# Two down projections of an f32 feed-forward kernel: the order of the operand forms in one, a second level of block products in the other

## The chip, the cores and the metric

The kernel runs on one core of a Trainium2 chip. The core has a matrix engine (TensorE, "PE" in the profile, with its weight loads as "PEld"), a vector engine (VectorE, DVE), a scalar engine (ScalarE, ACT), a general engine (GpSimd, POOL) and a queue engine (SyncE, SP). Each takes its instructions in order from a queue of its own, and they meet through semaphores. On-chip data lies in SBUF (128 partitions); TensorE writes its results into eight PSUM banks of 128 x 512 f32.

The metric is the device time of one launch in microseconds. The kernel before takes 685.91 us, the median of three runs (685.76 to 686.01).

## What is computed

1024 tokens (8 batches of 128) with 512 features pass through two residual layers. Cut to what matters:

```python
x = x + _L0_ffn_ref(_L0_cond_ref(x, ...), ...)     # 1: conditioner, then feed-forward
x = x + _L1_ffn_ref(_L1_cond_ref(x, ...), ...)     # 2: conditioner, then int4 feed-forward

def _L0_cond_ref(x, ...):                           # F = 1376, low-rank adapters of rank 16 by batch
    gate = lora_add(einsum('bnh,fh->bnf', x, W_gate), x, A_gate, B_gate)
    up   = lora_add(einsum('bnh,fh->bnf', x, W_up), x, A_up, B_up)
    act  = silu(gate) * up
    return lora_add(einsum('bnf,hf->bnh', act, W_down), act, A_down, B_down)

def _L0_ffn_ref(x, ...):                            # I = 1792, weights scaled by a rank-4 product
    d = silu(linear(x, gate_w, ...)) * linear(x, up_w, ...)
    return linear(d, down_w, ...)
```

The change concerns the two products with the down weights: `act` times `W_down` of the conditioner (1376 inputs, padded to 11 chunks of 128; 512 outputs; 1024 tokens), and `d` times `down_w` of the feed-forward (14 chunks of 128).

## The kernel before

**Layout.** Features lie on the 128 partitions, tokens on the free axis, so a matmul takes a 128 x 128 weight block (128 inputs, 128 outputs) and streams up to 512 tokens. Tokens come in two halves of 512 (`tb` 0 and 1), the 512 outputs in four blocks of 128 (`o`, or `m` and `m + 2` for the two halves of the outputs). Everything in these layers is f32.

**Seven products in place of eight.** Each projection is a 2 x 2 block product: inputs in two halves, outputs in two halves, tokens in two halves. It is made by the Winograd form of Strassen's scheme. With weights a11, a12, a21, a22 and tokens b11, b12, b21, b22, where the even chunks of the inputs are one half and the odd chunks the other, there are weight forms S1 = a21 + a22, S2 = S1 - a11, S3 = a11 - a21, S4 = a12 - S2, token forms T1 = b12 - b11, T2 = b22 - T1, T3 = b22 - b12, T4 = b21 - T2, and the products

- 1: a11 b11, 2: a12 b21, 3: S4 b22, 4: a22 T4, 5: S1 T1, 6: S2 T2, 7: S3 T3.

Outputs are sums of these; in the code products 2 and 3 are added by TensorE to the banks of 1 and 5, the others by DVE, ACT and POOL. A product is, for `m` in 0 and 1, one matmul of 128 x 512 per pair of chunks: 5 pairs in the conditioner (10 matmuls a product), 7 in the feed-forward (14). The conditioner's eleventh chunk has no partner; its products are made straight (`leftover`), and its low-rank adapters are added to the banks (`adapters`).

**The conditioner's down part** is `down` (L601), with `n = 11`. Forms are made on DVE: S1 of each pair at L302 while `weight_forms` is called with `later`, T3 into tiles of their own (`dt_c`, through `form`, L622 to L627), then T1, T2, T4 in place on the activations; the later weight forms S2, S4, S3 at L309, pair by pair (128 x 256). Product order: 1, the low-rank block of the down adapters (hook 1, tile `pt_d`), 2, 5, 3, 7, 6, 4. ACT copies product 1 to `du_c` (L672), products 2 and 3 to the output `h` (L669, L683), product 7 to `dv_c` (L701), POOL adds `dv_c` to `h` (L704), DVE adds the rest (L656, L707, L709, L710). Hook 6 makes the token forms of the next projection (L336) in the tiles `x`, whose contents are no longer needed by then; `x` is loaded again much later for the residual.

**The feed-forward's down part** is `down_second` (L716), with 14 chunks. Products 1, 5 and 6 are made as above. Products 2, 3, 7 and 4 go down one more level: six of their seven pairs are again a 2 x 2 block product (two groups of three pairs, two output blocks, two quarters of 256 tokens), made as seven parts of three matmuls of 128 x 256 (`of_blocks`, `part`), and the last pair is added with two matmuls of 128 x 512. The block that the second level shares (`z`, in bank `z1`) is copied by ACT after the parts 1, 6 and 7 (L809, L813, L817) into `r`; parts 6 and 7 add to the same bank after the copy before them. Their token forms come from DVE (`second_tokens`, L760), their weight forms from POOL (`second_weights`, through L302 and L309). DVE's order, written out by hand (L834 to L872): seven T3 after S1 of all pairs in one instruction, seven T1, then S2, S4, S3 of all pairs (128 x 1792), the tokens of product 2, of product 3, and so on. POOL gathers the adapters of the last conditioner and makes its weight forms in hook 2, after the weight forms of product 7; hook 3 turns scales on TensorE ahead of product 7. PE's order: 1, 5, 2, 3, 7, 6, 4.

**What sets the order.** Matmuls and most forms are wrapped in `in_order`, which keeps the order of the program on their engine; the rest is placed by a scheduler. Banks are eight, taken by `bank`; a bank is free when its last reader is done. After both down parts come the last conditioner (tiles `l`) and the int4 feed-forward (`gu_q`, `d_q`), whose weights POOL's queue loads (`load_q`, L1399 and L1401).

Of the kernel before, what the change touches and what calls it, by code (L numbers as in the profile page):

```python
# [7 lines left out]
F32 = mybir.dt.float32  # L8
# [3 lines left out]
ALU = mybir.AluOpType  # L12

P = 128
NB = 8
T = 1024
TB = 512
# [38 lines left out]
def kernel(  # L56
# [544 lines left out]
    def down(pool, layer: str, n: int, to, plus: bool, hooks, adapters=None):  # L601

        pairs = n // 2
        K2 = KC // 2
        blocks = {"11": 0, "12": 1, "21": 2, "22": 3}
        b = {
            w: [acts[2 * j + i // 2, i % 2] for j in range(pairs)] for w, i in blocks.items()  # L610
        }
        a = {i: [] for i in range(1, 8)}
        forms = []
        for j in range(pairs):
            wd = [ready[layer, "down", 2 * j + i] for i in range(2)]
            s = pool.tile([P, 3, H // 2], F32, tag=f"ds{j}", name=f"ds_{layer}{j}")
            halves = [w[:, bass.ts(i, H // 2)] for i in range(2) for w in wd]
            forms.append(weight_forms(nc.vector, *halves, *(s[:, i] for i in range(3)), True, later=True))
            for i, w in zip((1, 2, 7, 4, 5, 6, 3), (*halves, *(s[:, i] for i in range(3)))):
                a[i].append([w[:, bass.ts(m, P)] for m in range(K2)])  # L620

        def form(t: str, x1: str, x2: str, place):  # L622
            b[t] = []
            for j in range(pairs):
                out_ = place(j)
                in_order(nc.vector.tensor_tensor(out_, b[x1][j], b[x2][j], ALU.subtract))
                b[t].append(out_)  # L627

        def at(o: int, tb: int):
            return to[o][:, bass.ts(tb, TB)]  # L630

        banks = {}

        def sums(i: int, m: int, src: str, into=None, start=True, single=None, stop=True, goes_on=False):


            ps = banks[i, m] = bank(f"d{i}_{layer}{m}") if into is None else into
            alone = single is not None and n % 2
            product(ps, [w[m] for w in a[i]], b[src], start, stop and not alone, goes_on)
            if alone:  # L640
                leftover(ps, m, *single, False, stop, goes_on)
            return ps

        def leftover(ps, m: int, row: int, tb: int, start: bool, stop: bool, goes_on=False):
            wd = ready[layer, "down", n - 1]
            mm(
                ps, wd[:, bass.ts(m + 2 * row, P)], acts[n - 1, tb], start=start, stop=stop,
                skip_group_check=goes_on,
            )

        def hook(i: int):
            if i in hooks:
                hooks[i]()

        def plus_bank(o: int, tb: int, ps):
            nc.vector.tensor_tensor(at(o, tb), ps, at(o, tb), ALU.add)  # L656

        def temp(what: str, m: int):
            return pool.tile([P, TB], F32, tag=f"{what}{m}", name=f"{what}_{layer}{m}")

        u = [temp("du", m) for m in range(2)]
        v = [temp("dv", m) for m in range(2)]
        more = adapters is not None
        form("T3", "22", "12", lambda j: pool.tile([P, TB], F32, tag=f"dt{j}", name=f"dt_{layer}{j}"))
        def moved(o: int, tb: int, ps):
            if plus:
                plus_bank(o, tb, ps)
            else:
                nc.scalar.copy(at(o, tb), ps)  # L669

        for m in range(2):
            nc.scalar.copy(u[m], sums(1, m, "11"))  # L672
        hook(1)
        form("T1", "12", "11", lambda j: b["12"][j])
        for rest in forms:
            rest()
        for m in range(2):
            ps = sums(2, m, "21", banks[1, m], False, (0, 0), not more, True)
            if more:
                extra = bank(f"d8_{layer}{m}")  # L680
                leftover(extra, m, 1, 1, True, False)
                adapters(m, [[ps, None], [None, extra]], go_on={(0, 0)})
                nc.scalar.copy(at(m + 2, 1), extra)  # L683
            moved(m, 0, ps)
        for m in range(2):
            plus_bank(m + 2, 1, sums(5, m, "T1"))
        hook(5)
        for m in range(2):
            ps = sums(3, m, "22", banks[5, m], False, (0, 1), not more, True)
            if more:  # L690
                banks[4, m] = bank(f"d4_{layer}{m}")
                adapters(
                    m, [[None, ps], [banks[4, m], None]], fresh={(1, 0)}, more={(1, 0)},
                    go_on={(0, 1)},
                )
            moved(m, 1, ps)
        form("T2", "22", "T1", lambda j: b["22"][j])
        form("T4", "21", "T2", lambda j: b["21"][j])
        for m in range(2):
            ps = sums(7, m, "T3")  # L700
            nc.scalar.copy(v[m], ps)  # L701
            if plus:
                nc.gpsimd.tensor_tensor(at(m + 2, 0), at(m + 2, 0), v[m], ALU.add)
            nc.gpsimd.tensor_tensor(at(m + 2, 1), at(m + 2, 1), v[m], ALU.add)  # L704
        for m in range(2):
            ps = sums(6, m, "T2")
            nc.vector.tensor_tensor(u[m], ps, u[m], ALU.add)  # L707
            for o in (m, m + 2):
                nc.vector.tensor_tensor(at(o, 1), at(o, 1), u[m], ALU.add)  # L709
            nc.vector.tensor_tensor(at(m + 2, 0), at(m + 2, 0) if plus else v[m], u[m], ALU.add)  # L710
        hook(6)
        for m in range(2):
            ps = sums(4, m, "T4", banks.get((4, m)), not more, (1, 0))
            plus_bank(m + 2, 0, ps)

    def down_second(pool, act, hooks):  # L716

        pairs, thirds, quarter = NF // 2, NF // 4, TB // 2
        K2 = KC // 2
        ds = pool.tile([P, pairs, 3, H // 2], F32, tag="ds", name="ds_f")
        dt = pool.tile([P, pairs, TB], F32, tag="dt", name="dt_f")
        wd = [[wd_all[:, i::2, bass.ts(row, H // 2)] for i in range(2)] for row in range(2)]
        a = {
            1: wd[0][0], 2: wd[0][1], 7: wd[1][0], 4: wd[1][1],
            5: ds[:, :, 0], 6: ds[:, :, 1], 3: ds[:, :, 2],
        }  # L730
        b = {f"{i + 1}{tb + 1}": act[:, i::2, tb] for i in range(2) for tb in range(NTB)}
        b["T3"], b["T1"], b["T2"], b["T4"] = dt, b["12"], b["22"], b["21"]
        other_forms = weight_forms(nc.vector, *wd[0], *wd[1], *(a[i] for i in (5, 6, 3)), True, later=True)

        def form(t: str, x1: str, x2: str):
            for j in range(pairs):
                in_order(
                    nc.vector.tensor_tensor(b[t][:, j], b[x1][:, j], b[x2][:, j], ALU.subtract)  # L738
                )


        tokens2 = pool.tile([P, 4, thirds, quarter], F32, tag="tokens2", name="tokens2_f")
        own = [tokens2[:, i] for i in range(4)]
        b11 = [
            b["11"][:, i * thirds : (i + 1) * thirds, bass.ts(q, quarter)]
            for i in range(2) for q in range(2)
        ]
        groups = [slice(i * thirds, (i + 1) * thirds) for i in range(2)]
        second = {}

        def second_tokens(i: int, src: str, place, in_place: bool):

            b11, b12, b21, b22 = (
                b[src][:, group, bass.ts(q, quarter)] for group in groups for q in range(2)
            )
            t1, t2, t4, t3 = place
            if in_place:
                t3 = b12
            for to, x1, x2 in ((t1, b12, b11), (t2, b22, t1), (t4, b21, t2), (t3, b22, b12)):
                in_order(nc.vector.tensor_tensor(to, x1, x2, ALU.subtract))  # L760
            second["b", i] = {1: b11, 2: b21, 3: b22, 4: t4, 5: t1, 6: t2, 7: t3}

        def second_weights(i: int):
            a11, a12, a21, a22 = (
                a[i][:, group, bass.ts(m, P)] for m in range(2) for group in groups
            )
            s = pool.tile([P, 3, thirds, P], F32, tag="s2", name=f"s2_{i}", bufs=2)
            s1, s2, s4 = (s[:, n] for n in range(3))
# [3 lines left out]
        def at(o: int, tb: int):  # L772
            return x[o][:, bass.ts(tb, TB)]
# [1018 lines left out]
```

## Time and profile before

| | us |
|---|---|
| median of three runs | 685.91 (685.76 to 686.01) |
| the profiled execution, its own time | 684.2 |
| its span, first to last instruction | 682.4 |
| conditioner's down part on PE | 156.72 to 233.88 |
| feed-forward's gate and up on PE | 233.88 to 400.84 |
| feed-forward's down part on PE | 400.84 to 486.81 |
| last conditioner on PE | 486.81 to 517.89 |
| int4 feed-forward | 517.89 to the end |
| mean granted TensorE clock | 0.995 of full speed |

The profile is one execution. It gives busy time by engine, the chain of work that ended last, groups of equal instructions with their duration and the idle time before them, and a timeline. A matmul's end is modelled, so the distance between two starts is the safer duration. An f32 matmul of the program shows as two records. "x20" is a merged run of twenty records, and the bracket at the end of a line is the idle time of the engine before it and what ended it. In the stretches of 78 us around the conditioner's down part (156 to 234) DVE is busy 34.36 us, ACT 6.89 and POOL 2.53; from 430 to 490 DVE is busy 46.48 and POOL 45.11.

### The profile page before, as it was taken

The page shows a single profiled execution, that of the slowest core. Times are in us where ns is not written, and L with a number is a line of the kernel's source. Part 1 is how long each engine was busy: PE and PEld are TensorE (multiplying, and loading weights), DVE is VectorE, ACT ScalarE, POOL GpSimd, SP SyncE. Part 2 cuts the span into 40 slices and gives each one's busy share as a digit, 9 for nine tenths or more (in the row PEclk, how much of TensorE's full clock was granted, in tenths as well). Part 3 has the DMA queues.
Part 4 walks back from the last instruction along what each step waited for, and adds up shares of the span by engine and source line. Part 5 has one row for each costly group of instructions (what it writes and reads, how often), then busy time and mean ns, then how long its engine had stood idle before and what let it go on. Part 6 is the DMA issues. An engine that isn't in the chain of part 4 may idle for free.

```text
span 682.4 us, 7042 instructions
## 1 busy us (share of the span) xinstructions
PE 669.2 (98%) x2472; PEld 397.0 (58%) x2472; DVE 471.8 (69%) x637; ACT 189.7 (28%) x282; POOL 390.8 (57%) x343
## 2 busy tenths in 40 slices
PE   9999999999999999999999997999999999999995
PEld 3444444444444445666666653685636877788884
DVE  6545435434523586877878679886857888899997
ACT  1212112111101012334323320010114555656563
POOL 5357765340001045667866921488721998898996
PEclk9999999999999999999999998999999999999999
DMA  7501225030002002202200060000670130000003
GB/s 236 195 1 52 66 76 212 28 138 1 1 0 77 32 0 92 93 6 87 93 1 0 1 205 1 0 13 4 213 249 6 57 94 15 16 1 0 1 1 124
DMA packets 18335, 42.48 MB, mean 62 GB/s; under 512 B 3118, under 2 KB 4286, under 8 KB 18172
## 3 DMA queue, kind: packets, MB, share of 16 engines
q1 hardware_dynamic: 11772, 25.71, 10.7%
q0 software_dynamic: 5376, 14.49, 6.7%
q10 hardware_dynamic: 1152, 1.84, 0.8%
q8 instruction: 20, 0.33, 0.2%
q14 instruction: 15, 0.12, 0.1%
HBM read 39.93 MB, written 2.10 MB: 62 GB/s over the span
## 4 chain that ended last, share of the span: by engine, by line
PE 87%; POOL 6%; DVE 3%; issue 2%; ACT 1%; DVEq 0%; POOLq 0%; ACTq 0%
PE p_c L88 22%; PE p_f L88 15%; PE gu_q L1507 11%; PE d_c L88 11%; PE d_f L88 7%; PE d_q L1507 5%; PE l L88 4%; PE zb_f L88 3%; PE z L88 3%; PE za_f L88 3%; POOL sum L1522 2%; POOL x L1522 1%; PE bank L1507 1%; POOL act_lo L1522 1%; PE pw L88 1%
## 5 line engine op out<-in xcount | busy, mean ns | idle before, releaser
L1516 DVE SCALAR_TENSOR_TENSOR sum<-gu_q,sg,sum 128x1024 f32<-128x1024 f32 x65 | 83.2, 1283 | 15.4 <-ACT sum L1513 9.9
L1507 PE MATMUL gu_q<-h_hi,wgu_q 128*128 128x512 f32 x208 | 81.9, 394 | 0.5 <-DVE l_v L1451 0.4
L1507 PE MATMUL gu_q<-h_lo,wgu_q 128*128 128x512 f32 x208 | 81.1, 390 | 0.0
L88 PE MATMUL p_f<-x,s_f 128*128 128x512 f32 x112 | 52.2, 597 | 0.0
L1513 ACT ACTIVATE sum<-gu_q,sg 128x1024 f32<-128x1024 f32 x39 | 43.3, 1113 | 22.0 <-PE gu_q L1507 21.9
L1522 POOL TENSOR_TENSOR sum<-sum,sum 128x1024 f32<-128x1024 f32 (+1 forms) x14 | 32.6, 2328 | 23.9 <-DVE sum L1516 23.9
L1507 PEld LDWEIGHTS gu_q<-h_hi,wgu_q 128*128 128x128 f32 x208 | 39.0, 188 | 12.3 <-DVE x L1516 2.3
L1507 PEld LDWEIGHTS gu_q<-h_lo,wgu_q 128*128 128x128 f32 x208 | 39.1, 188 | 7.9
L589 DVE TENSOR_TENSOR act_c<-p_c,v_c 128x512 f32<-128x512 f32 x11 | 7.6, 691 | 52.2 <-PE p_c L88 52.2
L88 PE MATMUL p_c<-x,raw_c 128*128 128x512 f32 x88 | 43.3, 617 | 0.0
L1516 DVE SCALAR_TENSOR_TENSOR x<-d_q,sd,x 128x1024 f32<-128x1024 f32 x33 | 42.0, 1275 | 0.0
L88 PE MATMUL p_c<-T_x,raw_c 128*128 128x512 f32 x88 | 41.6, 595 | 0.0
L1522 POOL TENSOR_TENSOR act_lo<-sum,act_hi 128x1024 fp32r<-128x1024 f32 (+1 forms) x15 | 33.9, 2260 | 13.3 <-ACT act_hi L1574 13.3
L88 PE MATMUL p_c<-T_x,s_c 128*128 128x512 f32 x88 | 41.2, 592 | 0.0
L88 PE MATMUL p_f<-h,raw_f 128*128 128x512 f32 (+1 forms) x96 | 40.2, 541 | 0.1
L704 POOL TENSOR_TENSOR h<-h,dv_c 128x512 f32<-128x512 f32 x2 | 2.5, 1264 | 62.9 <-ACT dv_c L701 62.9
L590 POOL TENSOR_TENSOR act_c<-act_c,p_c 128x512 f32<-128x512 f32 x10 | 12.8, 1276 | 42.4 <-DVE act_c L589 33.0
L1507 PE MATMUL d_q<-act_hi,wd_q 128*128 128x512 f32 x88 | 34.9, 397 | 0.1
L1522 POOL TENSOR_TENSOR sum<-sum,sil_q 128x1024 f32<-128x1024 f32 (+1 forms) x15 | 34.0, 2266 | 1.6 <-ACT sil_q L1565 1.4
L1507 PE MATMUL d_q<-act_lo,wd_q 128*128 128x512 f32 x88 | 34.4, 391 | 0.0
L88 PE MATMUL d_f<-act_f,ds_f 128*128 128x512 f32 (+1 forms) x72 | 30.9, 584 | 3.5 <-DVE act_f L738 3.5
L88 PE MATMUL d_c<-act_c,wd 128*128 128x512 f32 x76 | 33.9, 596 | 0.0
(323 smaller groups left out, 1423.8 us busy)
## 6 DMA issues: line engine op xcount, KB each, us to landing
raw_f<-in_f_gu_dram SPq DMA_DIRECT2D x14, 512.0 KB
wgu_q<-in_q_gu_dram POOLq DMA_DIRECT2D x14, 512.0 KB, 7.5
raw_c<-in_c_gu_dram SPq DMA_DIRECT2D x10, 512.0 KB
wd<-in_f_down_dram SPq DMA_DIRECT2D x14, 256.0 KB
wd_q<-in_q_down_dram POOLq DMA_DIRECT2D x14, 256.0 KB, 7.5
x<-in_xT_dram SPq DMA_DIRECT2D x11, 256.0 KB
wd<-in_c_down_dram SPq DMA_DIRECT2D x11, 256.0 KB
out_dram<-x SPq DMA_DIRECT2D x6, 256.0 KB
```

The costliest lines, as they stand in the source:

```text
L88: in_order(nc_mm(*args, **kwargs))
L589: add(act[0], x4, v, ALU.add)
L590: mul(act[0], act[0], p1, ALU.mult)
L704: nc.gpsimd.tensor_tensor(at(m + 2, 1), at(m + 2, 1), v[m], ALU.add)
L1507: nc.tensor.matmul(ps, w, part[:, at], start=(n == 0), stop=(n == len(src) - 1))
L1513: in_order(nc.scalar.activation(to, ps, AF.Identity, scale=scale))
L1516: nc.vector.scalar_tensor_tensor(to, ps, scale, plus, op0=ALU.mult, op1=ALU.add)
L1522: in_order(nc.gpsimd.tensor_tensor(to, a, b, op))
```

## The change

`down_second` is removed, and one function `down` serves both layers in its form. It takes the activations as one tile (`act`, so `act_c` becomes one tile too), the first slot of its down weights in `wd_all` (`wd0`), and a list `dt` of tiles for one token form.

- T1 goes to `dt` (in the conditioner: five halves of the tiles `x`; in the feed-forward a tile of its own) and T3 is made in place on b12; before it was the other way round.
- S1 is made chunk by chunk, each chunk followed by its T1. The tokens of product 2 come next, then S2 and S4 (the code's `a[6]`, `a[3]`), the weight forms of product 2 on POOL, S3, and only after the tokens of product 3 the T3.
- The product order becomes 1, (hook 1), 5, 2, 3, 7, 6, 4 in both layers.
- In the conditioner the products 2, 3, 7 and 4 use `of_blocks` with groups of two pairs, the fifth pair and the single chunk with full matmuls, and the shared block's copies, `second_tokens` and `second_weights`, as in the feed-forward.
- POOL's second-level weight forms of product 4 come before hook 2 and not behind it; v is added to the output by DVE and not by POOL; in the conditioner POOL adds `r` to `h` for products 2 and 3.

The core of the diff:

```diff
-        form("T3", "22", "12")
-        form("T1", "12", "11")
-        other_forms()
+        for j in range(pairs):
+            added(nc.vector, a[5][:, j], wd[1][0][:, j], wd[1][1][:, j])
+            form_of(j, "T1", "12", "11")
         second_tokens(2, "21", own, False)
+        subtracted(a[6], a[5], a[1])
+        subtracted(a[3], a[2], a[6])
         second_weights(2)
-        banks1, banks5 = [], []
+        subtracted(a[7], a[1], a[7])
+        banks1, banks5, banks4 = [], [], None
         for m in range(2):
             banks1.append(sums(1, m, "11"))
             in_order(nc.scalar.copy(u[m], banks1[m]))
+        hook(1)
         for m in range(2):
             banks5.append(sums(5, m, "T1"))
-        second_tokens(3, "22", b11, False)
+        second_tokens(3, "22", dead, False)
         second_weights(3)
-        for m in range(2):
-            added(nc.vector, at(m + 2, 1), banks5[m], at(m + 2, 1))
-        onto_x(2, "21", banks1, 0)
+        form("T3", "22", "12")
+        if adapters is None:
+            for m in range(2):
+                added(nc.vector, at(m + 2, 1), banks5[m], at(m + 2, 1))
+            onto_output(2, "21", banks1, 0)
+        else:
+            def first_adapters(m: int):
+                extra = new(8, m)
+                leftover(extra, m, 1, 1, True)
+                adapters(m, [[banks1[m], None], [None, extra]], go_on={(0, 0), (1, 1)})
+                in_order(nc.scalar.copy(at(m + 2, 1), extra))
+                added(nc.vector, at(m + 2, 1), banks5[m], at(m + 2, 1))
+
+            onto_output(2, "21", banks1, 0, first_adapters)
         second_tokens(7, "T3", own, True)
         second_weights(7)
-        hooks[2]()
-        onto_x(3, "22", banks5, 1)
+        if adapters is None:
+            onto_output(3, "22", banks5, 1)
+        else:
+            banks4 = [new(4, m) for m in range(2)]
...
+            onto_output(3, "22", banks5, 1, second_adapters)
         second_weights(4)
+        hook(2)
         form("T2", "22", "T1")
         form("T4", "21", "T2")
-        second_tokens(4, "T4", b11, True)
-        hooks[3]()
+        second_tokens(4, "T4", dead, True)
+        hook(3)
         banks7, v = of_blocks(7, "T3")
         for m in range(2):
             added(nc.vector, v[m], banks7[m], v[m])
-            for tb in range(NTB):
-                added(nc.gpsimd, at(m + 2, tb), at(m + 2, tb), v[m])
+            for tb in range(NTB) if plus else (1,):
+                added(nc.vector, at(m + 2, tb), at(m + 2, tb), v[m])
         for m in range(2):
             added(nc.vector, u[m], sums(6, m, "T2"), u[m])
-            for o, tb in ((m, 1), (m + 2, 1), (m + 2, 0)):
-                added(nc.vector, at(o, tb), at(o, tb), u[m])
-        banks4, r = of_blocks(4, "T4")
+            for o in (m, m + 2):
+                added(nc.vector, at(o, 1), at(o, 1), u[m])
+            added(nc.vector, at(m + 2, 0), at(m + 2, 0) if plus else v[m], u[m])
+        hook(6)
+        banks4, r = of_blocks(4, "T4", banks4, (1, 0))
```

And where the two parts are called:

```diff
-        act_c = pool(c_layer, "act_c", "right", 2 * NF0)
+        act_c = pool(c_layer, "act_c", "right").tile([P, NF0, NTB, TB], F32, tag="act", name="act_c")
...
+            dt = [x[j // 2][:, bass.ts(j % 2, TB)] for j in range(NF0 // 2)]
             down(
-                pool(top, "down_c", "right"), "c", NF0, h, False,
+                pool(top, "down_c", "right"), "c", NF0, act_c, NF - NF0, h, False, dt,
                 {1: down_low_rank, 6: three_forms}, down_adapters,
             )
...
-        down_second(
-            pool(top, "down_f", "right"), act_all, {2: for_last_conditioner, 3: turn_scales}
-        )
+        down_f = pool(top, "down_f", "right")
+        dt = down_f.tile([P, NF // 2, TB], F32, tag="dt", name="dt_f")
+        down(
+            down_f, "f", NF, act_all, 0, x, True, [dt[:, j] for j in range(NF // 2)],
+            {2: for_last_conditioner, 3: turn_scales},
+        )
```

The function for one product by second-level blocks, with the new leftover, and its use onto the output:

```diff
-        def of_blocks(i: int, src: str, onto=None):
+        def of_blocks(i: int, src: str, onto=None, single=None):
...
             for m in range(2):
                 mm(
-                    to[m], a[i][:, pairs - 1, bass.ts(m, P)], b[src][:, pairs - 1],
+                    banks[m], a[i][:, pairs - 1, bass.ts(m, P)], b[src][:, pairs - 1],
                     start=onto is None, stop=True, skip_group_check=onto is not None,
                 )
+                if single is not None and n % 2:
+                    leftover(banks[m], m, *single)
...
+        def onto_output(i: int, src: str, banks, tb: int, more=lambda m: None):
+            banks, r = of_blocks(i, src, banks, (0, tb))
             for m in range(2):
-                added(nc.vector, at(m, tb), banks[m], at(m, tb))
+                more(m)
+                if plus:
+                    added(nc.vector, at(m, tb), banks[m], at(m, tb))
+                else:
+                    in_order(nc.scalar.copy(at(m, tb), banks[m]))
             for m in range(2):
                 added(nc.gpsimd, at(m, tb), at(m, tb), r[m])
```

## The prediction, made before the run

> **What bounds the kernel now.** I read the page first: the span, the busy shares and the chain that ended last by engine.
>
> ```profile
> span 682.4 us, 7042 instructions
> PE 669.2 (98%) x2472; PEld 397.0 (58%) x2472; DVE 471.8 (69%) x637; ACT 189.7 (28%) x282; POOL 390.8 (57%) x343
> ...
> PE 87%; POOL 6%; DVE 3%; issue 2%; ACT 1%; DVEq 0%; POOLq 0%; ACTq 0%
> ```
>
> TensorE (PE) is busy 98% of the time and 87% of the chain. So time is won only by giving PE less to do, or by closing holes in its row, and a new load on another engine costs something only if PE comes to wait for it. Then I read the timeline of PE over the two down parts (start, length, what, count, and in brackets the idle time before it):
>
> ```profile
> 206.31 8.85 PE L88 MATMUL d_c<-dt_c,wd 128*128 128x512 f32 x20
> 215.00 8.75 PE L88 MATMUL d_c<-act_c,ds_c 128*128 128x512 f32 x20
> 223.58 10.46 PE L88 MATMUL d_c<-act_c,wd 128*128 128x512 f32 x24
> 233.88 1.88 PE L88 MATMUL p_f<-h,raw_f 128*128 128x512 f32 x4
> ...
> 400.84 12.18 PE L88 MATMUL d_f<-act_f,wd 128*128 128x512 f32 x28
> 416.48 13.95 PE L88 MATMUL d_f<-act_f,ds_f 128*128 128x512 f32 x28 [3.46 <-DVE act_f L738]
> 430.27 1.88 PE L88 MATMUL d_f<-act_f,wd 128*128 128x512 f32 x4
> 431.99 1.46 PE L88 MATMUL z<-act_f,wd 128*128 128x256 f32 x6
> 433.28 1.46 PE L88 MATMUL z<-tokens_f,s 128*128 128x256 f32 x6
> ```
>
> An f32 product instruction appears as two records, so a first-level product of the conditioner (5 chunks, 2 output blocks) is x20. Starts tell the price: x20 takes 215.00 - 206.31 = 8.69 us, 0.43 us a record. x6 of the half-wide form takes 433.28 - 431.99 = 1.29 us, 0.215 us a record: half the columns, half the time. The conditioner's part has no hole (156.72 to 233.88). The feed-forward part has one, before product 5. The table by stretches (PE, PEld, DVE, ACT, POOL busy; the granted clock behind them) shows that it costs more than its 3.46 us:
>
> ```profile
> 413.00:417.00 4.00, 0.54 (x2) 0.30 (x2) 4.00 (x8) 0.58 (x1) 0.00 (x0) 0.98 0.00 0
> 417.00:420.50 3.50, 3.50 (x6) 1.45 (x5) 3.50 (x6) 0.00 (x0) 0.00 (x0) 0.54 0.02 5
> 420.50:430.00 9.50, 9.50 (x24) 4.24 (x23) 9.40 (x6) 0.00 (x0) 5.90 (x3) 1.00 0.00 0
> ```
>
> After the hole PE runs at a granted clock of 0.54 for 3.5 us. And DVE's own row says why PE waited:
>
> ```profile
> 409.50 2.02 DVE L302 TENSOR_TENSOR ds_f<-wd 128x1792 f32<-128x1792 f32 x1
> 411.44 4.30 DVE L738 TENSOR_TENSOR dt_f<-act_f 128x512 f32<-128x512 f32 x7
> 415.65 4.30 DVE L738 TENSOR_TENSOR act_f<-act_f 128x512 f32<-128x512 f32 x7
> ...
> 425.80 1.75 DVE L760 TENSOR_TENSOR tokens_f<-act_f 128x768 f32<-128x768 f32 x1
> 461.81 0.95 DVE L760 TENSOR_TENSOR act_f<-act_f 128x768 f32<-128x768 f32 x1
> ```
>
> DVE is free for this part at 409.50. It makes S1 in one piece, seven T3 that product 7 needs only at 453, and then the T1 that product 5 needs at once.
>
> **The change, part by part.**
>
> *Feed-forward, T1 ahead of T3, S1 by chunks.* A pair S1 chunk + T1 chunk costs DVE 0.34 (five S1 of 128x256 at L302 in the conditioner: 1.76 us) + 0.61 (4.30/7) = 0.95 us. From 409.50 chunk j is ready at 409.50 + 0.95(j+1): 410.45 for the first, 416.15 for the last. PE ends product 1 at 400.84 + 28 x 0.43 = 412.9 and needs chunk j at 412.9 + 0.86j, 418.1 for the last: never late. Product 5 then ends at 412.9 + 12.05 = 424.95, where the next group starts at 430.27 now. Gain 5.3 us: 3.5 hole, 1.7-1.8 slow clock. If the hole cost only itself it would be 3.5, the lower bound; above 5.3 nothing is left to win.
>
> [...]
>
> What goes late instead? The T3 move behind the tokens of products 2 and 3. DVE from 416.15: tokens of 2 (four of 128x768, 0.87 to 1.75 each), S2, S4, S3 (three of 128x1792 at 1.94), tokens of 3 (four), seven T3: 416.15 + 3.5 + 5.8 + 7.0 + 4.3 = 436.8, with 1.75 for the tokens of 3, which stand beside POOL. Product 2 runs on PE from 424.95 to 435.7, product 3 to 446.5, the two scale turns to 447.8, and product 7 needs T3 there: 11 us to spare. The second-level tokens of 7 (four more, up to 7 us) are ready by 447 with the x additions between, needed from 450.8: 4 us to spare. T2 and T4 (14 x 0.61 = 8.5 after product 3's r at 446) are there by 456, needed at 458.6. On POOL the in-place form of product 2 waits for S4 (423.5) and takes 1.0 to 2.71 us, needed at 433. The gathers and last-conditioner forms move behind product 4's forms and take 19.4 us now (451.33 to 470.7); put from 457 they end at 477, their readers start at 485. The load of the next weights behind them then issues at 477, now 482.98, and its readers run at 518. So all of it is covered. The additions of v go from POOL to DVE (4 x 0.61 = 2.4 us), in DVE's free 6.45 us before 480.
>
> *Conditioner, four of seven products by second-level blocks.* Pairs 5, groups of 2: a product of 20 records becomes 4 full records (the fifth pair) + 7 x 2 x 2 = 28 half-wide ones: 4 x 0.43 + 28 x 0.215 = 7.74 us against 8.69 (8.6 at 0.43). Gain 0.86 to 0.95 each, four of them: 3.5 us. Leftover chunks and adapters keep their number.
>
> What it adds: on POOL, idle here from 151 to 211, 16 weight forms of 128x256 (0.73 each in the gate-up units) and two more additions (1.26), 14 us; on DVE 12 second-level token forms on own or dead places and 4 in place (0.61 each, 9.8), 4 r additions and 4 more h additions (4.9). DVE is busy 34.4 of 78 us now. On PE each product gets two waits for an ACT copy of the shared block. The first has 4 + 4 records (1.7 us) as cover. The second has only part 3, four records, 0.86 us, where the feed-forward has six, 1.29. The copy starts 0.2 us after the last start of its block and takes 0.37 (ACT at 437.37 in the feed-forward), 0.57 in all: 0.29 us are left. Without that cover it would cost at most 0.57 x 4 = 2.3 us, so this term lies between 1.2 and 3.8; I take 3.5, since the cover is of measured rows.
>
> Due times, on the old clock: T1 (in dead x tiles) from 160.05 at 0.94 a pair is done at 164.8, even at twice that 169.5; product 5 starts at 170.4, behind the low-rank block. Product 2 by blocks runs at 179 to 188.5, its forms are done by 175. Product 7 starts at 204, its POOL forms stand behind two additions that end at 194 and take 3 us (11 at 2.7 each): 205 at worst, needed at 206.5. T2 waits for product 3's last reader (201.8) and is done at 205, T4 at 208, needed 211.7 and 220. Product 4 ends at 230.4 and the T forms of the next layer come in the same order as now.
>
> [...] The row: 128x768 takes 0.95 on DVE alone, 1.75 beside POOL. [...]
>
> **Sum.** 5.3 + 3.5 = 8.8 us. The profiled execution is 684.2 us with a span of 682.4: span 673.6, time 675.4. The median shown is 685.91, 1.7 above that execution; from it 677.1.
>
> **Rivals.**
> 1. *The conditioner's waits eat its gain.* If the ACT copies or POOL's forms come late by 0.5 us or more in every product, PE stops there in four places, each too short for the slow clock. For it: 0.29 us of cover. Against: the same chain in the feed-forward shows no hole. Gain 5.3 + 0 to 1.2: 679.4 to 680.6.
> 2. *The hole moves or was cheaper.* Product 5 starts early, but PE then waits at product 2's or 7's forms, or timed runs do not lose the slow clock as the profiled one did: 3.5 + 3.5 = 7.0 or less, 678.9 to 681.
> 3. *Slower.* DVE becomes the bound of the feed-forward part: if its operations take 1.75/0.95 of their time throughout, tokens of 2, three S, tokens of 3 and seven T3 take 7 + 10.7 + 7 + 7.9 = 32.6, T3 ends at 448.8, additions and tokens of 7 follow by 459 against 450.8, T2 and T4 take 15.7 to 475 against 467, product 4's tokens another 7. Two stops of about 8 us, each with 1.7 us of slow clock: +19 - 8.8, about 10 us slower at worst, 696; it turns from a total of 8.8 us of waits. For it: 1.75 us beside POOL. Against: POOL works some 19 us between 424 and 451 now, so DVE cannot be beside it all the time.
> 4. *The gain goes off behind the part.* The end of the kernel is another stage (from 518 on) that starts when the last conditioner has finished; if that waited for POOL's weights, nothing would come through: 685.9. The loads issue 35 us ahead, so hardly.
>
> **Chances.** Forecast (gain 7.5 to 9.5) 0.78; rivals 1 and 2 together 0.13; rival 4 0.03; rival 3 0.06. The predicted time is 677.1. The forecast's own range is 676.2 to 678.6; taking in rivals 1 and 2 and 0.6 us below for a chip or day that differs, 675.6 to 680.6. A measurement of this kernel can tell 0.2% (1.4 us) from no change: faster 0.91, same 0.03, slower 0.06.
>
> **What would show it.** Right: no idle time on PE before product 5 (now dt_f), a clock of 1.00 through that stretch, product 5 ending 12 us after product 1; the conditioner's part 73.6 us long instead of 77.2, with x28 half-wide records in about 6.0 us per product; POOL's forms long before their readers. Wrong: idle time in brackets before a z or d_c group with ACT or POOL behind it, a clock under 1.00 after it, or tokens of 7 on DVE ending after product 7's start.

## The result, and the profile after

| | us |
|---|---|
| before, median of four runs beside the changed kernel | 685.84 (684.66 to 686.01) |
| after, median of four runs | 678.06 (678.03 to 678.41) |
| ratio after / before | 0.9892, 95% interval 0.9876 to 0.9907 |
| the profiled execution after, its own time and span | 678.08 and 676.4 |

The change made the kernel 7.8 us faster. The stretches on PE, as starts of the first matmul of each part, before and after:

| part on PE | before | after |
|---|---|---|
| conditioner's down part | 156.72 to 233.88: 77.16 us | 157.11 to 230.58: 73.47 us |
| gate and up of the feed-forward | 166.96 us | 166.95 us |
| feed-forward's down part | 400.84 to 486.81: 85.97 us | 397.53 to 480.69: 83.16 us |
| last conditioner | 31.08 us | 31.14 us |

So 3.69 us come out of the conditioner and 2.81 out of the feed-forward; all else kept its length to 0.1 us. The profiled spans differ by 6.0, since the conditioner's part began 0.39 later in this execution. The page after, its head, the busy line and the chain by engine:

```profile
span 676.4 us, 7209 instructions
...
PE 664.3 (98%) x2520; PEld 405.1 (60%) x2520; DVE 501.2 (74%) x661; ACT 193.8 (29%) x292; POOL 408.8 (60%) x357
...
PE 84%; DVE 6%; POOL 6%; issue 2%; DMA 1%; ACT 1%; SPq 0%; POOLq 0%; DVEq 0%; ACTq 0%
```

PE is still busy 98% of the time. But DVE's share of the chain went from 3% to 6%, though the hole before product 5 was to go. The list of PE's waits has a new first line (us in total, times, longest):

```profile
PE d_f L88 <- DVE x L627: 2.3, 1, 2.3
```

One wait of 2.3 us for DVE's addition onto `x`. Where it stands is seen in PE's timeline of the feed-forward part after (start, length, what, count, idle time before it):

```profile
397.53 12.18 PE L88 MATMUL d_f<-act_f,wd 128*128 128x512 f32 x28
409.55 12.18 PE L88 MATMUL d_f<-dt_f,ds_f 128*128 128x512 f32 x28
421.56 1.88 PE L88 MATMUL d_f<-act_f,wd 128*128 128x512 f32 x4
...
431.05 1.46 PE L88 MATMUL d_f<-tokens_f,wd 128*128 128x256 f32 x6
434.83 1.98 PE L88 MATMUL d_f<-act_f,ds_f 128*128 128x512 f32 x4 [2.32 <-DVE x L627]
436.65 1.46 PE L88 MATMUL z_f<-act_f,ds_f 128*128 128x256 f32 x6
```

Product 5 (`dt_f`) now follows product 1 with no idle time, and 12.01 us later comes product 2. So the old hole is closed. Product 2 ends at 432.5, and product 3, the line with the bracket, starts only at 434.83. The stretches around it (PE, PEld, DVE, ACT, POOL busy; granted clock, DMA share, GB/s):

```profile
410.00:421.00 11.00, 11.00 (x27) 4.92 (x26) 10.90 (x14) 0.33 (x1) 0.37 (x1) 1.00 0.00 0
432.50:434.83 2.33, 0.01 (x1) 0.00 (x1) 2.33 (x5) 0.00 (x0) 0.00 (x0) 1.00 0.00 0
434.83:438.00 3.17, 3.17 (x11) 2.06 (x12) 3.17 (x5) 0.00 (x0) 1.29 (x2) 1.00 0.02 5
```

In the middle row PE does nothing, DVE works all the time, and ACT and POOL are idle. The clock is 1.00 before and behind this hole. What DVE works at is in its timeline:

```profile
413.73 1.95 DVE L630 TENSOR_TENSOR tokens_f<-act_f,tokens_f 128x768 f32<-128x768 f32 x2
...
420.47 2.02 DVE L630 TENSOR_TENSOR wd<-wd 128x1792 f32<-128x1792 f32 x1
422.40 11.77 DVE L630 TENSOR_TENSOR act_f<-act_f 128x768 f32<-128x768 f32 x11
434.10 1.27 DVE L627 TENSOR_TENSOR x<-d_f,x 128x512 f32<-128x512 f32 x2
```

The x11 are the four tokens of product 3 and the seven T3. Behind them stand the two additions of product 5's banks onto `x`. Product 3 adds onto these same banks (`onto_output(3, "22", banks5, 1)`), so PE may not write there before DVE has read them. The T3 are needed only for product 7, which starts at 447.01, 12.9 us after the last of them is done, but they stand in the queue ahead of a reading that the next product needs.

In the conditioner nothing waits. PE's timeline after, over product 2 by blocks:

```profile
179.47 3.60 PE L88 MATMUL d_c<-act_c,wd 128*128 128x512 f32 x8
182.90 1.03 PE L88 MATMUL z_c<-act_c,wd 128*128 128x256 f32 x4
...
188.08 1.03 PE L88 MATMUL d_c<-tokens_c,wd 128*128 128x256 f32 x4
188.94 1.02 PE L88 MATMUL d_c<-act_c,wd 128*128 128x512 f32 x2
```

The 28 half-wide records take 188.94 - 182.90 = 6.04 us, with no bracket between.

### The profile page after: what moved, and what is told of

It is laid out like the page before. It is cut to its first block, busy times and chain, and to the rows that moved or that the text cites. A ratio compares the mean times of both kernels' runs of the same rounds, so it can differ in the third digit from the quotient of the medians.

```text
span 676.4 us, 7209 instructions
## 1 busy us (share of the span) xinstructions
PE 664.3 (98%) x2520; PEld 405.1 (60%) x2520; DVE 501.2 (74%) x661; ACT 193.8 (29%) x292; POOL 408.8 (60%) x357
## 4 chain that ended last, share of the span: by engine, by line
PE 84%; DVE 6%; POOL 6%; issue 2%; DMA 1%; ACT 1%; SPq 0%; POOLq 0%; DVEq 0%; ACTq 0%
PE p_c L88 21%; PE p_f L88 15%; PE gu_q L1450 12%; PE d_c L88 8%; PE d_q L1450 5%; PE d_f L88 4%; PE l L88 4%; PE zb_f L88 3%; PE za_f L88 3%; PE z_f L88 2%; PE z_c L88 2%; DVE act_f L630 1%; POOL sum L1465 1%; PE bank L1450 1%; POOL act_lo L1465 1%
## 5 line engine op out<-in xcount | busy, mean ns | idle before, releaser
L88 PEld LDWEIGHTS p_f<-x,s_f 128*128 128x128 f32 x112 | 20.9, 190 | 19.5 <-issue 16.3
L88 PEld LDWEIGHTS p_c<-T_x,s_c 128*128 128x128 f32 x88 | 16.7, 190 | 21.0 <-issue 19.6
L88 PEld LDWEIGHTS p_c<-T_x,raw_c 128*128 128x128 f32 x88 | 16.6, 190 | 21.3 <-issue 19.7
```

Source lines behind the costliest of these rows:

```text
L88: in_order(nc_mm(*args, **kwargs))
```

## The experiments

All times are medians beside runs of the kernel before on the same chip: 684.69 (23 runs, 682.86 to 686.35) for the first four, 684.76 (13 runs, 684.53 to 686.36) for the others, which ran on another chip. The changed kernel ran with neither group, so its distance from the experiments is also given by lengths in the profiled executions.

| run | us (range, runs) | ratio to before, 95% |
|---|---|---|
| e1_read_first | 675.73 (675.38 to 675.91, 4) | 0.9868 [0.9851, 0.9884] |
| e2_f_alone | 682.44 (682.04 to 684.14, 12) | 0.9975 [0.9965, 0.9985] |
| e3_c_alone | 680.71 (679.22 to 681.69, 6) | 0.9935 [0.9920, 0.9950] |
| e4_before_again | 684.40 (682.90 to 685.23, 12) | 0.9991 [0.9980, 1.0001] |
| d0_hole_1 | 677.17 (677.10 to 677.26, 4) | 0.9885 [0.9869, 0.9902] |
| d2_hole_4 | 682.00 (681.60 to 683.75, 4) | 0.9953 [0.9937, 0.9970] |
| d3_hole_6 | 684.67 (684.15 to 685.54, 10) | 0.9997 [0.9987, 1.0006] |
| e5_no_cover | 682.03 (681.91 to 682.15, 4) | 0.9956 [0.9939, 0.9973] |

### The reading of product 5's banks ahead of the T3

```diff
         second_weights(3)
-        form("T3", "22", "12")
         if adapters is None:
             for m in range(2):
                 added(nc.vector, at(m + 2, 1), banks5[m], at(m + 2, 1))
+            form("T3", "22", "12")
             onto_output(2, "21", banks1, 0)
         else:
+            form("T3", "22", "12")
```

In the branch of the conditioner the order stays as it was.

> The changed kernel with one move: in the feed-forward DVE adds product 5's two banks to the output ahead of the seven T3, not behind them. Theory A (the hole of 2.32 us before product 3 is the wait for DVE's reading of product 5's banks, onto which product 3 adds, and this reading stood behind tokens of 3 and seven T3): no idle time before product 3, span 676.4 - 2.3 = 674.1, time 675.7. Rival B (the hole is the wait for an operand of product 3, its S4, tokens or b22, or for DVE slowed beside POOL): the hole stays at 2 us or more, time 678.0. Rival C (T3 comes too late now and the hole moves to product 7): idle time before product 7's first matmul, 676 to 678.

Measured: 675.73 us, 2.33 less than the changed kernel. PE's timeline of this run, and the stretches at the place of the hole:

```profile
431.50 1.46 PE L88 MATMUL d_f<-tokens_f,wd 128*128 128x256 f32 x6
432.79 1.88 PE L88 MATMUL d_f<-act_f,ds_f 128*128 128x512 f32 x4
434.51 1.46 PE L88 MATMUL z_f<-act_f,ds_f 128*128 128x256 f32 x6
```

```profile
429.00:433.00 4.00, 4.00 (x20) 3.52 (x19) 4.00 (x7) 0.96 (x2) 1.49 (x1) 1.00 0.01 4
433.00:437.00 4.00, 4.00 (x16) 2.77 (x15) 4.00 (x8) 0.37 (x1) 0.62 (x1) 1.00 0.00 0
```

The bracket is gone and PE is busy throughout. DVE shows the order that makes it so:

```profile
422.85 6.77 DVE L630 TENSOR_TENSOR act_f<-act_f 128x768 f32<-128x768 f32 x4
429.55 1.27 DVE L627 TENSOR_TENSOR x<-d_f,x 128x512 f32<-128x512 f32 x2
430.75 4.29 DVE L630 TENSOR_TENSOR act_f<-act_f 128x512 f32<-128x512 f32 x7
```

The additions are done at 430.8, 2 us before product 3 starts at 432.79, and the seven T3 end at 435. The feed-forward's down part takes 80.57 us in place of 83.16, 5.40 less than before the change. The rivals written down ahead of the run, a late operand of product 3 or a new hole before product 7, are both excluded. So the order of these nine instructions is the whole cause of the hole, and nothing else comes late in its place. This version is the fastest of all that ran.

### Each part alone

In `e2_f_alone` the kernel before calls the new `down` for the feed-forward only and keeps its own for the conditioner. In `e3_c_alone` the changed kernel calls the old `down_second` for the feed-forward. `e4_before_again` is the kernel before, unchanged, to see how one kernel's runs spread.

```diff
-        down_second(
-            pool(top, "down_f", "right"), act_all, {2: for_last_conditioner, 3: turn_scales}
-        )
+        down_f = pool(top, "down_f", "right")
+        dt = down_f.tile([P, NF // 2, TB], F32, tag="dt", name="dt_f")
+        down_new(
+            down_f, "f", NF, act_all, 0, x, True, [dt[:, j] for j in range(NF // 2)],
...
```

(e2; e3 is the reverse on the changed kernel.)

> The kernel before with the new function for the feed-forward part alone, the conditioner's part as before. If the two parts add up: the feed-forward part on PE takes 83.2 us instead of 86.0, conditioner 77.2 as before, span 682.4 - 2.8 = 679.6. Its time is 681.4 by the profiled execution of before, and 678.06 + 3.7 = 681.8 counted from the changed kernel. Rival: the wins are not additive (DVE or POOL work of the one part reaches into the other), then the conditioner's stretch or the gate and up stretch of 166.95 us changes by more than 0.5 us.

> The changed kernel with the old function for the feed-forward part, so only the conditioner's part is changed. If the parts add up: conditioner 73.5 us on PE, the hole of 3.46 us and a clock near 0.54 behind it are back, span 682.4 - 3.7 = 678.7, time 680.5 by the profiled execution of before or 682.1 by the median of before; runs spread by up to 1.7 us, with a lower mean clock in the longer ones, if the slow clock after the hole lasts one window in some executions and two in others. Rival: the spread between 684.2 and 685.9 in the kernel before comes from elsewhere (DMA, start), then longer runs have the same mean clock.

> The kernel before against itself, to see its single executions with their clock. If the hole's slow clock is what makes 684.2 in one execution and 685.9 in others: two groups of times about 1.7 us apart, the longer with a mean clock lower by about 0.0025 (1.7 of 684). Rival (the 1.7 us come from the start or from DMA): one clock for both groups.

Measured, as lengths of the two down parts on PE in the profiled executions:

| run | conditioner | feed-forward |
|---|---|---|
| e4, kernel before | 77.16 | 85.96 |
| e2, feed-forward alone | 77.16 | 84.87 |
| e3, conditioner alone | 73.48 | 85.96 |
| changed kernel | 73.47 | 83.16 |
| e1 | 73.47 | 80.57 |

The parts don't touch each other: the conditioner's takes 77.16 or 73.47 to 73.48, whichever feed-forward follows. The feed-forward's part is 84.87 in e2 and 83.16 in the changed kernel (as e2 was expected to have) though the code and the hole are the same. Nor is e2 as fast as the 681.4 to 681.8 us that were expected, even in its lowest run. The difference of 1.71 us is seen behind the hole of e2, in PE's timeline and the stretches:

```profile
438.79 2.64 PE L88 MATMUL d_f<-act_f,ds_f 128*128 128x512 f32 x4 [2.34 <-DVE x L742]
441.22 2.54 PE L88 MATMUL z_f<-act_f,ds_f 128*128 128x256 f32 x6
443.60 1.46 PE L88 MATMUL z_f<-act_f,s_f 128*128 128x256 f32 x6
```

```profile
437.00:441.00 4.00, 2.21 (x4) 1.01 (x5) 4.00 (x7) 0.00 (x0) 0.32 (x1) 0.87 0.00 0
441.00:445.00 4.00, 4.00 (x14) 3.15 (x13) 3.93 (x4) 0.37 (x1) 4.00 (x3) 0.70 0.00 0
```

By starts the first two groups take 441.22 - 438.79 = 2.43 and 443.60 - 441.22 = 2.38 us; behind the same hole in the changed kernel's profile they take 1.82 and 1.30. That is 0.61 + 1.08 = 1.69 us lost to a granted clock of 0.87 and 0.70, in one execution and not in the other.

In slices of 0.5 us behind the hole, the granted clock is 0.50 for 3.42 us in e2, and for 3.41 to 3.42 us behind the old hole of 3.46 us in the profiles of before, e3 and e4; in those of the changed kernel and of e1 it is 1.00 throughout. This stretch is what e3's expectation calls a window. By estimate, half of 3.42 us, it costs 1.7 us where PE has work all through it (1.69 in e2's profile), and takes 0.0025 off the mean clock of a run of 682 us.

The single runs fall into levels that agree with this, by their mean clocks. Of e2's twelve, seven lie at 682.04 to 682.54 with a mean clock of 0.997 to 0.999 and four at 684.05 to 684.14 with 0.995. The twelfth, 683.62, has 0.997 like the low ones, so its 1.1 us can't be put down to the clock. Of the 23 runs of the kernel before, four lie at 682.86 to 683.89 (0.998), 16 at 684.22 to 684.94 (0.995 to 0.996) and three at 685.84 to 686.35 (0.994). In e3 the hole before product 5 is back (3.5 us in its list of waits) and with it the levels, two runs at 679.22 and 679.36 (0.998) and the others at 680.69 to 681.69 (0.995 to 0.996). All four runs of the changed kernel have a clock of 0.997 to 0.999; four are too few to say that its hole is never followed by a slow stretch.

The clock isn't the only source of spread. In the ten profiled executions the conditioner's down part begins anywhere from 156.72 to 158.42. The 685.23 us of e4 and the 684.20 of the profile before have the same slow stretch and the same down parts (77.16 and 85.96 or 85.97); e4's later start, 157.83 against 156.72, makes the difference. So the rival that was written down for e4, the start, holds for this part of the spread. Whether the runs above 685.8 had two slow stretches or one and a later start is not shown, as no profile of the kernel before has two.

### Holes of one, four and six microseconds

How long must a hole be to cost more than its length? The same place was made into holes of other lengths. `d0_hole_1` puts the reading behind five of the seven T3. `d2_hole_4` and `d3_hole_6` leave it behind all seven and form S2 once or twice more just ahead of it, the same values again, so no work is left out.

```diff
-        form("T3", "22", "12")
+        for j in range(pairs):
+            if adapters is None and j == 5:
+                for m in range(2):
+                    added(nc.vector, at(m + 2, 1), banks5[m], at(m + 2, 1))
+            form_of(j, "T3", "22", "12")
```

```diff
         if adapters is None:
+            for _ in range(2):
+                subtracted(a[6], a[5], a[1])
             for m in range(2):
                 added(nc.vector, at(m + 2, 1), banks5[m], at(m + 2, 1))
```

(d0 first; d3 second, with one repeat in d2.)

> The changed kernel with product 5's banks read on DVE after five of the seven T3, not after all: two T3 (2 x 0.61 us) less ahead of the reading. Theory A: hole before product 3 of 2.3 - 1.2 = 1.1 us, time 675.7 + 1.1 = 676.8, and no slow clock if a hole this short cannot halve it; 678.5 in an execution where it does. Rival B (operand wait): hole stays at 2.3 us.

> The changed kernel with one S2 of 128x1792 made a second time on DVE ahead of the reading of product 5's banks (same values, 1.94 us). Theory A: hole of 2.3 + 1.9 = 4.3 us; 675.7 + 4.3 = 680.0 without a slow clock, 681.7 with one stretch of 3.4 us at half clock, 683.4 with two. If the slow clock comes with the length of the hole, no execution is at 680.0. Rival: the hole's cost is its length alone, all executions at 680.

> The changed kernel with S2 made twice more ahead of the reading of product 5's banks (2 x 1.94 us). Theory A: hole of 6.2 us; 681.9 without slow clock, 683.6 with one stretch at half clock, 685.3 with two; one or two in every execution. Rival: all at 681.9.

The line behind the hole in PE's timeline, of d0, of d2 and of d3:

```profile
433.89 1.98 PE L88 MATMUL d_f<-act_f,ds_f 128*128 128x512 f32 x4 [1.12 <-DVE x L627]
```

```profile
438.11 3.78 PE L88 MATMUL d_f<-act_f,ds_f 128*128 128x512 f32 x4 [4.28 <-DVE x L627]
441.69 2.12 PE L88 MATMUL z_f<-act_f,ds_f 128*128 128x256 f32 x6
```

```profile
439.32 3.78 PE L88 MATMUL d_f<-act_f,ds_f 128*128 128x512 f32 x4 [6.32 <-DVE x L627]
442.90 2.56 PE L88 MATMUL z_f<-act_f,ds_f 128*128 128x256 f32 x6
```

The same four records take 1.98 us behind 1.12 us of idle time and 3.78 behind 4.28 and 6.32. The clock of d2 there, and of d3:

```profile
434.00:438.00 4.00, 0.00 (x0) 0.00 (x0) 4.00 (x6) 0.00 (x0) 0.00 (x0) 0.77 0.00 0
438.00:442.00 4.00, 3.89 (x5) 1.82 (x6) 4.00 (x6) 0.00 (x0) 2.00 (x2) 0.50 0.00 0
442.00:446.00 4.00, 4.00 (x17) 3.39 (x17) 3.93 (x4) 0.37 (x1) 3.92 (x3) 0.87 0.00 0
```

```profile
438.00:442.00 4.00, 2.67 (x3) 1.17 (x4) 4.00 (x7) 0.00 (x0) 0.79 (x1) 0.54 0.00 0
442.00:446.00 4.00, 4.00 (x12) 2.88 (x11) 3.93 (x3) 0.37 (x1) 4.00 (x3) 0.61 0.00 0
```

In both profiles the clock is at 0.50 for 6.83 us, twice as long as behind the old hole. It begins while PE is still idle, at 436.2 in d2 and 438.3 in d3.

Against e1, which has no hole here, by medians, and by the length of the feed-forward's down part in the profile (e1 80.57), which leaves the start of the kernel out:

| hole in the profile | time over e1 | beyond the hole's length | runs over 1 us above e1 plus the hole | part over e1's, profile |
|---|---|---|---|---|
| 1.12 (d0) | 1.44 | 0.32 | none of 4 | 1.39 |
| 2.32 (changed kernel) | 2.33 | 0.01 | none of 4 | 2.59 |
| 4.28 (d2) | 6.27 | 2.0 | all 4 | 6.97 |
| 6.32 (d3) | 8.94 | 2.6 | all 10 | 9.45 |

By the last column a hole without slow clock cost 0.27 us more than its bracket (d0 and the changed kernel alike); beyond that d2 lost 2.4 us and d3 2.9 to the clock. (In e2, with its hole of 2.34 us, five of twelve runs lie 1.1 us or more above the other seven, four of them with a lower mean clock.) That a hole costs its length and no more falls with d2 and d3: no run of d2 is near 680.0 and none of d3 near 682.1. A hole of 6.3 us gives back the whole gain of the change (684.67 against 684.76).

### The cover of ACT's copy taken away

On e1: part 3 of each product by blocks, which PE runs while ACT copies the shared block, goes behind part 7, which waits for the copy. It is the same work in another order, in all eight products.

```diff
             part(z, 6)
             in_order(nc.scalar.copy(r[:, 1], z))
-            part(banks[0][:, right], 3)
             part(z, 7)
             in_order(nc.scalar.copy(r[:, 2:4], z.unsqueeze(1).to_broadcast([P, 2, quarter])))
+            part(banks[0][:, right], 3)
             part(banks[1][:, left], 4)
```

> The kernel with the reading moved up (675.73) and, in both layers, part 3 put behind part 7: nothing lies between part 6 and part 7 on PE, and part 7 waits for ACT's copy of the shared block. By the prediction's row the way from part 6's last start through the copy is 0.57 us: eight products, 8 x 0.4 to 0.57 = 3.2 to 4.6 us, time 679 to 680.3, idle time on PE before each seventh part behind ACT. Rival (the copy is overlapped in another way and no cover is needed): 675.7.

Measured: 682.03 us, 6.30 over e1, or 0.79 for each of eight products; 3.2 to 4.6 in all was expected. PE's timeline in the conditioner, and two lines of the list of waits:

```profile
185.69 1.03 PE L88 MATMUL z_c<-tokens_c,s_c 128*128 128x256 f32 x4
187.27 1.10 PE L88 MATMUL z_c<-tokens_c,wd 128*128 128x256 f32 x4 [0.55 <-ACT r_c L722]
188.21 1.03 PE L88 MATMUL d_c<-act_c,s_c 128*128 128x256 f32 x4
```

```profile
PE z_c L88 <- ACT r_c L722: 2.2, 4, 0.6
PE z_f L88 <- ACT r_f L722: 1.7, 3, 0.6
```

The list names ACT's copy in seven of the eight places. In the eighth, product 7 of the feed-forward, it names a form of POOL, which ended 0.02 us after the copy; the bracket there is 0.55 as well.

The bracket says 0.55, but by starts the place costs more: 187.27 - 185.69 = 1.58 where such a group takes 0.86, and the next group 0.94, together 0.80. So the round trip from PE over ACT's copy and back, with nothing to cover it, costs PE 0.79 us: part 7 starts 0.72 us late and the group behind it loses the rest. How much part 3 hides is seen in ACT's timeline, first of the changed kernel, where part 7 starts at 187.22, then of e5, where it starts at 187.27:

```profile
186.55 0.37 ACT L722 COPY r_c<-z_c 128x256 f32<-128x256 f32 x1 [2.22 <-PE z_c L88]
```

```profile
186.76 0.37 ACT L722 COPY r_c<-z_c 128x256 f32<-128x256 f32 x1 [2.22 <-PE z_c L88]
```

With the cover the copy ends 0.30 us before part 7 starts, without it 0.14 us before. So the 0.86 us of part 3 in the conditioner hide the 0.72 us with about 0.15 to spare, and the 1.29 us in the feed-forward with 0.57.

## Why the prediction came out as it did

**The conditioner's term held.** 3.69 us were measured where 3.5 were taken, and the records behaved as priced: 6.04 us for 28 half-wide ones. Its rival, waits for ACT's copies or POOL's forms, did not come: no bracket stands in this part. Stops of about the 0.5 us that it names left the clock alone in e5: from 430 to 450, with two stops of 0.55 us, each stretch of 4 us is at 1.00, and all four runs have a mean clock of 0.999. But the cover was mis-sized. The prediction counted 0.57 us up to the end of the copy and 0.29 us to spare. It left out the way back: in e5 PE starts 0.14 us after the copy's end, so 0.72 us have to be covered and half of the margin was there. (Its 0.2 us run from the start of the next group, 437.17 to 437.37, and not from the last start of the block, as it says; the cover counts from the same point, so the sum isn't touched by this.)

The added POOL work stands beside DVE's, and some operations of both took longer there. In the trace of the changed kernel a 128x256 form takes 1.18 us on POOL at 195.56, beside DVE (0.73 in the gate-up rows of the kernel before), and a 128x512 operation of DVE at 194.41, beside POOL, 1.74 (0.68 elsewhere). Not all do: the form at 158.01 takes 0.73 beside DVE. All this stays hidden, as no PE wait for POOL stands in this part.

**The feed-forward's term was half right.** Closing the hole before product 5 gave what the prediction said: in e1's profile the part is 5.40 us shorter than in the profile before, against 5.3. The changed kernel got 2.81 of it. The step that failed is the paragraph "What goes late instead? The T3 move behind the tokens of products 2 and 3". Its times were good. It had the T3 end at 436.8 on the old clock; they ended at 434.10 + 3.3 = 437.4, with the 3.3 us that the part starts earlier. It had product 2 end at 435.7; it ended at 432.5 + 3.3 = 435.8. But it asked only when the T3's own reader needs them (product 7, "11 us to spare"), and mentioned the x additions behind them only in passing, as something that comes before the tokens of 7. It did not ask who waits for these additions. By its own numbers the answer was there: additions ready at 436.8 + 1.2 = 438.0, product 3 due at 435.7, a hole of 2.3 us. Rival 2, that the hole moves, came in kind, but it looked at the forms of products 2 and 7 and not at the banks of product 5.

**The slow clock was a term with several values, and the number came out well in part by luck.** The prediction took 1.7 to 1.8 us from one profiled execution. That is right for this execution, but runs of the kernel before at 682.9 with a mean clock of 0.998 show hardly any, and most runs show about 1.7. From the profiled 684.2 the sum gave 675.4, and the new hole of 2.3 us with the part's later start of 0.39 would make it 678.1. The prediction then added 1.7 us for the distance between that execution and the median, which did not carry over to the changed kernel. What this distance was is open: the clocks of those three runs are not on record, but the profile before has the earliest start of all ten, so a later start can be as much as a second slow stretch. The hole that was missed and the 1.7 us that were added nearly cancelled, and so 677.1 came within 1 us of 678.06.

The measured gain divides by the profiles into 3.69 us for the conditioner, 3.46 - 2.32 = 1.14 for the shorter hole, and 1.67 for the slow clock that the profile before has and the one after has not: 6.50 together. The other 1.3 us up to the 7.78 between the medians are not shown by a profile. Three of the four runs of the kernel before lay high there, at 685.76 to 686.01; against the 684.69 of the 23 runs the gain would be 6.6.

**The other rivals did not occur.** DVE did not become the bound: after the hole PE never waits for DVE in this part again, and DVE's operations took what was taken for them (in e1, four tokens of product 3 in 6.77 us, 1.69 each, against 1.75). Nor did the gain go off behind the part: the last conditioner takes 31.14 us as against 31.08, and POOL issues the next weights at 475.74, far ahead of their readers at 512.

## What to carry to other kernels

When instructions move back in a queue, list everything that now stands behind them, and for each the reader and the next writer of its place: an engine that reads a bank also holds up the product that will add onto that bank, here for 2.32 us. Put such a reading as soon as its bank is full and let forms with a late reader follow; here the order of nine instructions was worth 2.3 us. Price a hole from several executions: behind 2.3 us the slow clock cost nothing in the changed kernel and 1.7 us in e2's profile. And take the starting point of a forecast from many runs, since three of them lay 1.2 us above the median of 23.

## What the runs showed of the hardware

- The clock fell behind a hole shorter than the one of 3.46 us too. Behind 2.34 us it fell to 0.50 in e2's profile, and by time and mean clock in 4 of its 12 runs (0.995 against 0.997 to 0.999); behind 2.32 us in the changed kernel's profile it stayed at 1.00; behind 1.12 us it fell in none of 4 runs (0.997 to 0.999), and by their times behind 4.28 and 6.32 us in all 14 (0.990 to 0.997). So the length of the hole alone did not decide it.
- The slow clock came in stretches of one length or twice that: 3.41 to 3.42 us at 0.50 in four profiles, 6.83 us in two. They began at no fixed distance from the hole: 2.4 us into it in d2, 5.3 us into it in d3, 0.3 us behind it in the profile before and 1.2 us behind it in e2. What sets the beginning is not shown.
- A wait's bracket said less than the wait cost. In e5 the brackets are 0.55 us and each place costs 0.79, as the bracket counts from the modelled end of the group before, 0.17 us after its successor would have started, and the group behind it took 0.94 us by starts in place of 0.86. The same holds for the hole before product 3: the four records behind it take 1.82 us by starts and 1.72 without it, and the part is 2.59 us longer for a bracket of 2.32.
